# Layer 2 of a four-layer image kernel: the crossing pixel lines copied inside SBUF by ScalarE instead of fetched by transfers

## The chip, the cores and the metric

The kernel runs on one core of a Trainium2 chip. The metric is the device time of one execution in microseconds (us). The kernel before took 3193.68 us, the median of 3 runs (3190.29 to 3196.78). One further execution was profiled; the trace, and every duration read from it, belong to that one.

## The reference

1024 images of 16x16 pixels and 16 channels, float32, pass through four layers, each of the form x = x + layer(groupnorm(x)), with 8 groups of 2 channels:

```python
x = x + _L0_conv_ref(_gn(x), core0, core1, core2)   # a matrix given as a tensor train
x = x + _L1_conv_ref(_gn(x), ...)                   # cellular automaton: Sobel filters, 48->128->16, mask
x = x + _L2_conv_ref(_gn(x), filters, bias)         # 3x3 convolution, 16 -> 16 channels, plus bias
x = x + _L3_conv_ref(_gn(x), ...)                   # cellular automaton again
```

The change is in layer 2 alone: a 3x3 convolution with zero padding at the borders, plus a bias. Each output pixel needs its eight neighbours, so also the pixels one column to the left and right.

## The kernel before

The batch is split into two chunks of 512 images; `X0` and `X1` hold one chunk each in SBUF as [128 partitions, 32 lines, 512 images]. The four layers come one after another, and within a layer chunk 0, then chunk 1. What lies in DRAM between the layers is `xf[layer][chunk]`.

*Layout in layer 2.* A row of an image, 16 columns of 16 channels, is 256 numbers, and a line has only 128 partitions. So the image is cut into a left and a right half (`wh` 0 and 1) of 8 columns: line 16*wh + h holds row h of half wh. Partition 32*m + 2*c + v is column 2*m + v of the half and channel c. All columns of a half are thus on the partition axis, and a 128x128 matrix mixes columns and channels at once.

*The convolution, `layer_conv` (L1138).* For each row h there are two PSUM banks, one a half (6 banks, so three rows can be under way). `inner` (L1160) multiplies lines h-1, h and h+1 of the half by one 128x128 matrix each: three matmuls a half, two at the upper and lower border. In the trace every f32 matmul is two records. The one column that the neighbour half must deliver is not in these lines. `across` (L1169) adds it: a small matmul on a tile `hx`, whose rows 64*wh + 16*y + c hold the other half's border column of row h + y - 1, 48 rows a half. Its output is only the 32 rows of the outermost pair of columns (rows 96 to 127 for the left half, 0 to 31 for the right one). `halo(k)` fills the tile hx for image rows 4k to 4k+3 by DMAs from X to the tile, issued on the sync queue: L1153, and L1156 for the row that the border repeats. There are 48 and 4 of them in the two chunks. Three hx tiles take turns.

*The end of a row, `finish`.* ScalarE (L1191) adds the bias and brings a bank to an SBUF tile r, of which six take turns. GpSimd then issues a DMA (L1192) that adds r onto `xf[2][n]` in DRAM, where x lies already. So the sum x + layer stays in DRAM, and the next user must wait for these transfers.

*What sets the order.* `layer_conv` gives 54 steps: for each pair of rows `first`, `inner`, `first`, `inner`, then `across` for both, then `last` for both. `run` (L1423) goes through them and weaves other work in between: the loads of a list on the sync queue, spread over the first `by` share of the steps, and the steps of a background computation placed by their costs within a span, given as two shares of the layer. On each engine the instructions then run in the order in which they were written. The norms are the background:
- beside the convolution of X0: the 16 loads of X1 (`load_wc`, L766, 512 KB each) and `norm_lines(X1)`: VectorE sums over the lines (L592 and L589), `pmean` on PE (L675), the copy m by ScalarE (L636), 16 subtractions on VectorE (L621), 16 squares by ScalarE (L606) with their sums on VectorE (L592), `pvar` on PE (L679), a reciprocal root (L653, L659 to L663), 16 multiplications (L621);
- beside the convolution of X1: the weights of layer 3 (`put(L3)`), the 16 loads of X0 for layer 3 (`load_cw`, L773) out of what layer 2 has just added up, and `norm_cw(X0)`. That one goes by four quarters of the columns: pmean (L704), m, subtractions, squares and pvar (L708) for each, then one root, then `pr` on PE (L720), which spreads it, and the multiplications by quarter.

The squares' tiles have three buffers, one of which holds the running sum. Layer 3 begins with matmuls on X0 (L1410), whose results ScalarE brings to the tiles hid (L1413), and second matmuls on those (L1263). Layer 1 has the same form; its last operations are L1312 and L1313 on GpSimd and the store L1315 on the sync queue.

Of the kernel before, what the change touches and what calls it, by code (L numbers as in the profile page):

```python
# [12 lines left out]
ALU = mybir.AluOpType  # L13
# [5 lines left out]
B, S, C = 1024, 16, 16  # L19
P = 128  # L20
NB = 512
# [82 lines left out]
def conv_preact_kernel(ctx: ExitStack, tc: tile.TileContext, a: dict, out: bass.AP):  # L104
    nc = tc.nc
    V, A, G, T = nc.vector, nc.scalar, nc.gpsimd, nc.tensor
# [9 lines left out]
    xf = [  # L116
        [dram.tile([8, 4, P, NB], F32, tag=f"xf{l}_{n}", name=f"xf{l}_{n}") for n in range(NCH)]
        for l in range(5)
    ]
# [16 lines left out]
    def work(shape, tag, name, dt=F32):  # L136
        p, sizes = pool["sb"]
        return p.tile(shape, dt, tag=tag, name=name, bufs=sizes[tag])
# [38 lines left out]
    for hf in range(2):  # L177
        rows = slice(64 * hf, 64 * hf + 64)
# [231 lines left out]
    convw = cst("convw", [P, 448])  # L410

    def conv_weights():


        room = work([P, 2, NB], "t4", "convn").rearrange("p a b -> p (a b)")
        fn = room[:, 0:384].rearrange("p (y w o) -> p y w o", y=3, w=8)
        hn = room[:, 384:400]
        fw = convw[:, 0:384].rearrange("p (y w o v) -> p y w o v", y=3, w=4, v=2)
        hw = convw[:, 384:448].rearrange("p (e o v) -> p e o v", e=2, v=2)
        V.memset(room[:, 0:400], 0.0)  # L420
        V.memset(hw, 0.0)
        f = a["L2_conv_filters"]
        with nc.allow_non_contiguous_dma(reason="weights"):
            for w in range(8):
                for kw in range(3):
                    if 0 <= w + kw - 1 < 8:
                        wi = w + kw - 1
                        G.dma_start(
                            fn[32 * (wi // 2) + wi % 2 : 32 * (wi // 2) + 32 : 2, :, w],
                            f[:, kw].rearrange("y i o -> i y o"),  # L430
                        )
            for wh in range(2):
                for y in range(3):
                    r0 = 64 * wh + 16 * y
                    G.dma_start(hn[r0 : r0 + 16], f[y, 2 - 2 * wh])
            for m in range(4):
                for v in range(2):
                    G.dma_start(
                        b2[32 * m + v : 32 * m + 32 : 2], a["L2_conv_bias"].unsqueeze(1)
                    )  # L440

        def spread():
            for y in range(3):
                V.tensor_copy(fw[:, y], fn[:, y].rearrange("p (w v) o -> p w o v", v=2))
            for wh in range(2):
                rows = slice(64 * wh, 64 * wh + 64)
                for e in range(2):
                    V.tensor_copy(hw[rows, e, :, 1 - wh], hn[rows])
                V.memset(hw[64 * wh : 64 * wh + 16, 1], 0.0)

        return spread

# [311 lines left out]
    def load_wc(X, src):  # L764
        return [
            lambda wh=wh, h=h: nc.sync.dma_start(X[:, 16 * wh + h : 16 * wh + h + 2], rows_wc(src, wh, h, 2))  # L766
            for wh in range(2)
            for h in range(0, S, 2)
        ]

    def load_cw(X, src):
        return [
            lambda q=q, w=w: nc.sync.dma_start(  # L773
                X[:, 8 * q + w : 8 * q + w + 2], src[w : w + 2, q].rearrange("w p b -> p w b")
            )
            for q in range(4)
            for w in range(0, 8, 2)
        ]
# [5 lines left out]
    def rows_wc(t, wh, h, n=1):  # L784

        t = t[4 * wh : 4 * wh + 4].rearrange("w q (c h) b -> (w q c) h b", h=S)
        return t[:, h : h + n]
# [182 lines left out]
    def layer_train():  # L970
# [160 lines left out]

    conv = dict(
        fw=convw[:, 0:384].rearrange("p (y m) -> p y m", y=3),
        hw=convw[:, 384:448].rearrange("p (e m) -> p e m", e=2),
    )

    def layer_conv(X, n):

        st = {}

        def start():
            halo(0)

        def halo(k):
            t = st["h", k] = work([P, 4, NB], "hx", "hx")
            for wh in range(2):
                src = X[slice(97, 128, 2) if wh else slice(0, 32, 2), 16 * (1 - wh) : 16 * (1 - wh) + 16]
                for y in range(3):  # L1150
                    r0, h0 = 64 * wh + 16 * y, 4 * k + y - 1
                    lo, hi = max(h0, 0), min(h0 + 4, S)
                    nc.sync.dma_start(t[r0 : r0 + 16, lo - h0 : hi - h0], src[:, lo:hi])  # L1153
                    if lo > h0:

                        nc.sync.dma_start(t[r0 : r0 + 16, 0:1], src[:, 0:1])  # L1156

        def inner(h, y):
            for wh in range(2):
                T.matmul(  # L1160
                    st["po", h][wh], conv["fw"][:, y], X[:, 16 * wh + h + y - 1],
                    start=y == max(0, 1 - h), stop=y == min(2, S - h),
                )

        def across(h):
            rows = 32 if h == S - 1 else 48
            for wh in range(2):
                cols = slice(0, 32) if wh else slice(96, 128)
                T.matmul(  # L1169
                    st["po", h][wh][cols], conv["hw"][64 * wh : 64 * wh + rows, h == 0],  # L1170
                    st["h", h // 4][64 * wh : 64 * wh + rows, h % 4], start=False, stop=False,
                )

        def first(h):
            if h % 2 == 0 and h > 0:
                finish(h - 1)
            if h % 4 == 1 and h + 4 < S:
                halo(h // 4 + 1)
            st["po", h] = [bank([P, NB], "o", "po2") for _ in range(2)]
            inner(h, max(0, 1 - h))  # L1180

        def last(h):
            inner(h, min(2, S - h))
            if h % 2 == 0 or h == S - 1:
                finish(h)

        def finish(h):

            for wh in range(2):
                r = work([P, NB], "r", "conv")  # L1190
                A.activation(r, st["po", h][wh], AF.Identity, bias=b2)  # L1191
                G.dma_start(rows_wc(xf[2][n], wh, h), r.unsqueeze(1), accum_op=ALU.add)  # L1192

        steps = []
        for h in range(0, S, 2):
            for j in (h, h + 1):
                steps.append(lambda j=j: first(j))
                if 0 < j < S - 1:
                    steps.append(lambda j=j: inner(j, 1))
            steps += [  # L1200
                lambda h=h: (across(h), across(h + 1)), lambda h=h: last(h), lambda h=h: last(h + 1)
            ]
        return start, steps
# [219 lines left out]
    def run(layer, us, loads, *spans, by=0.0):  # L1423

        start, main = layer
        start()
        loads, done = list(loads), 0  # L1430
        todo = []
        for bg, lo, hi in spans:
            bg = [b if isinstance(b, tuple) else (1, b) if callable(b) else (b, None) for b in bg]
            idle = sum(b[0] for b in bg if b[1] is None) / (us * (hi - lo))
            less = min(1.0, 0.7 / idle) if idle else 1.0
            weight = sum(b[0] for b in bg if b[1] is not None)
            at = lo
            for cost, step in bg:
                if step is None:
                    at += cost * less / us  # L1440
                else:
                    todo.append((at, step))
                    at += (hi - lo) * (1 - idle * less) * cost / weight
        todo.sort(key=lambda x: x[0])
        for i, step in enumerate(main):
            step()
            part = (i + 1) / len(main)
            while done < len(loads) and done < len(loads) * part / (by or 1e-9):
                loads[done]()
                done += 1  # L1450
            while todo and (todo[0][0] < part or i == len(main) - 1):
                todo.pop(0)[1]()

    def put(L):
        return lambda: nc.sync.dma_start(pack, L["pack"])

    X0, X1 = XN
# [60 lines left out]
    last = alone(N, 3) + rstd(nst, slice(96, 128)) + [3] + scaled(N, [3])  # L1518
    nca_sb = dict(t4=2, s=3, n=2, wq=5, mask=1, f=5, hid=8, u=2, r=4, nx=1)
    nca_ps = dict(h=6, o=2)  # L1520
    conv_sb, conv_ps = dict(gn, s=3, r=6, hx=3), dict(o=6, m=2)
    on_vector[0] = True
    with ExitStack() as es:
        shared[0] = "o"
# [8 lines left out]
    with ExitStack() as es:  # L1533
        shared[0] = "m"
        stage(es, conv_sb, conv_ps)
        run(layer_conv(X0, 0), 108, load_wc(X1, xf[2][1]), (norm_lines(X1), 0.09, 1.1), by=0.12)
        run(
            layer_conv(X1, 1), 108, [put(L3)] + load_cw(X0, xf[3][0]), (norm_cw(X0, True), 0.09, 1.04), by=0.12
        )
    with ExitStack() as es:  # L1540
        shared[0] = "o"
# [41 lines left out]
```

## Time and profile before

| what | value |
|---|---|
| median of 3 runs | 3193.68 us |
| the profiled execution's own time | 3191.8 us |
| its span from first to last instruction | 3190.1 us |
| TensorE clock granted, mean | 0.98 |
| layer 2, first L1160 matmul to the first matmul of layer 3 | 2339.7 to 2591.5 us |
| busy in layer 2: PE, VectorE, ScalarE, GpSimd | 216.8, 158.5, 78.5, 57.1 us |
| L1160: records in layer 2, from start to start | 368, 0.43 us |
| L1169: records, eight in a row | 128, 1.84 us |
| ScalarE: a square of 128x1024 (L606), a result of 128x512 (L1191) | 1.05, 0.69 us |
| VectorE: a subtraction or a sum of 128x1024 in this stage | 1.22 us |
| loads of X1 (L766): first issue | 2349.9 us |
| accumulating transfers of layer 2 (L1192): issue on GpSimd, to landing | 0.95, 6.1 us |

The table's rows are read so. The span is a little less than the execution's own time, and a change inside the span moves both alike. "Busy" is time in which an engine executes an instruction; a PE whose clock is lowered is busy too, only slower. An idle engine costs time only when the work that ends last waits for it. The waits of an engine are named by what ended them: "PE pmean L675 <- DVE s1s L596" is idle time of PE before its matmul into pmean, which ended when VectorE had finished s1s. "SPq" is the sync engine's DMA queue, DVE is VectorE, ACT is ScalarE, POOL is GpSimd, PEld is the loading of weights into TensorE.

### The profile page before, as it was taken

The page shows a single profiled execution, that of the slowest core. Times are in us where ns is not written, and L with a number is a line of the kernel's source. Part 1 is how long each engine was busy: PE and PEld are TensorE (multiplying, and loading weights), DVE is VectorE, ACT ScalarE, POOL GpSimd, SP SyncE. Part 2 cuts the span into 40 slices and gives each one's busy share as a digit, 9 for nine tenths or more (in the row PEclk, how much of TensorE's full clock was granted, in tenths as well). Part 3 has the DMA queues.
Part 4 walks back from the last instruction along what each step waited for, and adds up shares of the span by engine and source line. Part 5 has one row for each costly group of instructions (what it writes and reads, how often), then busy time and mean ns, then how long its engine had stood idle before and what let it go on. Part 6 is the DMA issues. An engine that isn't in the chain of part 4 may idle for free.

```text
span 3190.1 us, 37179 instructions
## 1 busy us (share of the span) xinstructions
PE 3058.5 (96%) x13874; PEld 1260.3 (40%) x13874; DVE 1785.6 (56%) x2378; ACT 1018.3 (32%) x1690; POOL 670.6 (21%) x706
## 2 busy tenths in 40 slices
PE   7899899999999999999999999999979899999996
PEld 5444333444444444444444433333323233333332
DVE  5255345755554555544556678558757647754222
ACT  4331221100001000000111166666624356655553
POOL 1116532200000000000000034435432124432221
PEclk8999999999999999999999999999989999999998
DMA  7535545443333433322222254454476765433445
GB/s 283 201 142 97 121 101 160 133 144 104 104 109 132 146 116 104 104 98 96 90 95 90 76 168 133 129 167 154 139 192 110 185 139 173 136 92 115 128 137 186
DMA packets 243299, 424.77 MB, mean 133 GB/s; under 512 B 37844, under 2 KB 91952, under 8 KB 239408
## 3 DMA queue, kind: packets, MB, share of 16 engines
q1 hardware_dynamic: 217824, 368.63, 35.5%
q0 software_dynamic: 24480, 53.48, 8.3%
q8 instruction: 110, 1.80, 0.2%
q14 instruction: 69, 0.57, 0.1%
q10 hardware_dynamic: 816, 0.30, 0.0%
HBM read 238.78 MB, written 165.60 MB: 127 GB/s over the span
## 4 chain that ended last, share of the span: by engine, by line
issue 46%; PE 31%; POOL 8%; DMA 4%; DVE 2%; SPq 1%; ACT 1%; POOLq 0%; DVEq 0%; ACTq 0%
PE ph L1410 11%; PE po L1078 10%; PE po L1263 4%; POOL res L1313 4%; POOL u L1312 4%; PE po L1160 2%; DMA xn<-xf 1%; PE L_conv_pe L382 1%; SPq L941 1%; DVE xn L621 1%; DMA hx<-xn 1%; PE pw L1001 1%; PE ptout L948 1%; DVE sq L592 1%; POOL L_conv_wy L394 0%
## 5 line engine op out<-in xcount | busy, mean ns | idle before, releaser
L1078 PE MATMUL po<-xn,w 128*128 128x512 f32 x3584 | 1584.3, 598 | 4.6 <-DVE xn L892 4.6
L1078 PEld LDWEIGHTS po<-xn,w 128*128 128x128 f32 x3584 | 669.9, 190 | 852.6 <-issue 833.7
L1413 ACT ACTIVATE hid<-ph,pack 128x512 f32<-128x512 f32 x1024 | 653.9, 686 | 429.2 <-PE ph L1410 308.4
L1114 DVE TENSOR_TENSOR r<-r,po 128x512 f32<-128x512 f32 x576 | 377.8, 683 | 499.0 <-PE po L1078 476.3
L1312 POOL TENSOR_TENSOR u<-u,mask 128x512 f32<-128x512 f32 x128 | 202.5, 1582 | 1858.9 <-DMA nx<-xn 1241.7
L1410 PE MATMUL ph<-xn,wq 32*128 32x512 f32 x3664 | 573.1, 613 | 1.5 <-DMA wq<-L_conv_wy 1.5
L1006 ACT COPY w<-pw 128x512 f32<-128x512 f32 (+1 forms) x320 | 150.6, 558 | 1194.0 <-issue 970.4
L1410 PEld LDWEIGHTS ph<-xn,wq 32*128 32x128 f32 x3664 | 228.6, 184 | 263.3 <-issue 231.4
L1410 PE MATMUL ph<-xn,pack 32*128 32x512 f32 x1288 | 302.2, 631 | 4.5 <-ACT hid L1413 3.2
L1263 PE MATMUL po<-hid,pack 128*32 128x512 f32 x2048 | 283.0, 609 | 1.2 <-DVE u L1275 0.9
L1019 DVE TENSOR_TENSOR w<-w 128x512 f32<-128x512 f32 x320 | 211.2, 684 | 115.2 <-ACT w L1006 114.7
L621 DVE TENSOR_TENSOR xn<-xn,m 128x1024 f32<-128x1024 f32 x160 | 225.9, 1461 | 47.1 <-ACT m L636 47.1
L1313 POOL TENSOR_TENSOR res<-res,u 128x512 f32<-128x512 f32 x128 | 215.2, 1681 | 17.0 <-PE po L1263 2.7
L1275 DVE SCALAR_TENSOR_TENSOR u<-po,pack,xn 128x512 f32<-128x512 f32 x128 | 95.9, 749 | 157.6 <-PE po L1263 150.9
L1160 PE MATMUL po<-xn,convw 128*128 128x512 f32 x368 | 168.5, 609 | 0.0
L1410 PEld LDWEIGHTS ph<-xn,pack 32*128 32x128 f32 x1288 | 114.5, 187 | 100.7 <-issue 61.7
L1114 DVE TENSOR_TENSOR xn<-xn,po 128x512 f32<-128x512 f32 x96 | 64.3, 684 | 125.9 <-PE po L1078 125.8
L592 DVE TENSOR_TENSOR sq<-sq 128x1024 f32<-128x1024 f32 x78 | 110.6, 1418 | 15.2 <-ACT sq L606 12.0
L1263 PEld LDWEIGHTS po<-hid,pack 128*32 128x32 f32 x2048 | 42.9, 108 | 189.7 <-issue 137.4
L394 POOL DMA_DIRECT2D L_conv_wy<-xn x160 | 89.0, 563 | 99.0 <-ACT xn L152 90.7
L1160 PEld LDWEIGHTS po<-xn,convw 128*128 128x128 f32 x368 | 69.3, 193 | 99.3 <-issue 96.7
L592 DVE TENSOR_TENSOR s<-s,xn 128x1024 f32<-128x1024 f32 x60 | 86.4, 1441 | 29.1 <-DMA xn<-xf 27.9
(163 smaller groups left out, 1776.9 us busy)
## 6 DMA issues: line engine op xcount, KB each, us to landing
xf<-r SPq DMA_DIRECT2D x112, 512.0 KB, 3.8
xn<-xf SPq DMA_DIRECT2D x96, 512.0 KB, 5.1
r<-xf SPq DMA_DIRECT2D x80, 512.0 KB, 4.5
wq<-L_conv_wy SPq DMA_DIRECT2D x192, 192.0 KB, 2.8
res<-xf SPq DMA_DIRECT2D x128, 256.0 KB, 3.0
xf<-res SPq DMA_DIRECT2D x96, 256.0 KB, 2.0
res<-xr SPq DMA_DIRECT2D x256, 64.0 KB, 2.8
xf<-conv POOLq DMA_DIRECT2D x64, 256.0 KB, 6.1
```

The source lines that it names most:

```text
L592: return lambda: V.tensor_tensor(st["t"], st["t"], p(), ALU.add)
L621: V.tensor_tensor(part, part, m().unsqueeze(1).broadcast_to([P, 2, NB]), op)
L1006: A.copy(w[:, k0:4, :, 32 * r : 32 * r + 32].rearrange("p k t (v o) -> p v (k t) o", v=2), pw[r],)
L1019: V.tensor_tensor(w[:, k], w[:, x], w[:, y], ALU.add if sign > 0 else ALU.subtract)
L1078: T.matmul(po, st["w", u][:, matrix, t], x, start=t == 0, stop=t == 3)
L1114: V.tensor_tensor(r[at], r[at], po, ALU.add if sign > 0 else ALU.subtract)
L1160: T.matmul(st["po", h][wh], conv["fw"][:, y], X[:, 16 * wh + h + y - 1], start=y == max(0, 1 - h), stop=y == min(2, S - h),)
L1263: T.matmul(po[32 * j : 32 * j + 32], nca["w1"][:, v], hid[j], start=v == 0, stop=v == 1)
L1312: G.tensor_tensor(u, u, st["m"][:, w2], ALU.mult)
L1313: G.tensor_tensor(r, r, u, ALU.add)
L1410: T.matmul(ph, w, x, start=k == 0, stop=k == len(tiles) - 1)
L1413: A.activation(h, ph, AF.Relu, bias=nca["bt"][:, r : r + 1])
```

## The change

- The tile hx holds two image rows for both halves, [96, 2 halves, 2 rows, 512]: rows 32*y to 32*y + 31 are a full pair of columns (both columns, 16 channels) of row h + y - 1. ScalarE fills it with six copies a tile, each 32 partitions by up to 1024 elements, from X's partitions 0 to 31 or 96 to 127. No DMA is left in it. GpSimd clears the row above the upper border in the first tile.
- The weights for it are laid out anew: 96 rows for each half, with zeros for the column of the pair that isn't the neighbour. The matmul of `across` is 96 rows by 32 columns in place of 48 by 32.
- Tiles 0 and 1 are filled at the start of a chunk, tile h/2 + 2 at `first(h)` of each even h, ahead of the `finish` of the row before.
- `finish` puts its accumulating DMAs in a list, from which GpSimd issues them later; twelve r tiles in place of six.
- The loads are spread over the first 0.07 of the steps in place of 0.12, the layer-3 weights come behind the loads of X0, and the norms' spans end at 1.08 and 1.1 in place of 1.1 and 1.04.

```diff
@@ conv_weights
-        hn = room[:, 384:400]
+        hn = room[:, 384:416].rearrange("p (n o) -> p n o", n=2)
...
-                    r0 = 64 * wh + 16 * y
-                    G.dma_start(hn[r0 : r0 + 16], f[y, 2 - 2 * wh])
+                    G.dma_start(hn[32 * y + wh : 32 * y + 32 : 2, wh], f[y, 2 - 2 * wh])
...
-                rows = slice(64 * wh, 64 * wh + 64)
-                for e in range(2):
-                    V.tensor_copy(hw[rows, e, :, 1 - wh], hn[rows])
-                V.memset(hw[64 * wh : 64 * wh + 16, 1], 0.0)
+                V.tensor_copy(hw[:, wh, :, 1 - wh], hn[:, wh])
@@ layer_conv
         def start():
             halo(0)
+            halo(1)
 
         def halo(k):
-            t = st["h", k] = work([P, 4, NB], "hx", "hx")
-            for wh in range(2):
-                src = X[slice(97, 128, 2) if wh else slice(0, 32, 2), 16 * (1 - wh) : 16 * (1 - wh) + 16]
-                for y in range(3):
-                    r0, h0 = 64 * wh + 16 * y, 4 * k + y - 1
-                    lo, hi = max(h0, 0), min(h0 + 4, S)
-                    nc.sync.dma_start(t[r0 : r0 + 16, lo - h0 : hi - h0], src[:, lo:hi])
-                    if lo > h0:
-
-                        nc.sync.dma_start(t[r0 : r0 + 16, 0:1], src[:, 0:1])
+            if k >= S // 2:
+                return
+            t = st["h", k] = work([96, 2, 2, NB], "hx", "hx")
+            if k == 0:
+                G.memset(t[0:32, :, 0], 0.0)
+            for y in range(3):
+                lo, hi = max(2 * k + y - 1, 0), min(2 * k + y + 1, S)
+                at = lo - (2 * k + y - 1)
+                for wh in range(2):
+                    A.copy(
+                        t[32 * y : 32 * y + 32, wh, at : at + hi - lo],
+                        X[96 * wh : 96 * wh + 32, 16 * (1 - wh) + lo : 16 * (1 - wh) + hi],
+                    )
@@
         def across(h):
-            rows = 32 if h == S - 1 else 48
+            rows = slice(0, 64 if h == S - 1 else 96)
             for wh in range(2):
                 cols = slice(0, 32) if wh else slice(96, 128)
                 T.matmul(
-                    st["po", h][wh][cols], conv["hw"][64 * wh : 64 * wh + rows, h == 0],
-                    st["h", h // 4][64 * wh : 64 * wh + rows, h % 4], start=False, stop=False,
+                    st["po", h][wh][cols], conv["hw"][rows, wh], st["h", h // 2][rows, wh, h % 2],
+                    start=False, stop=False,
                 )
 
         def first(h):
-            if h % 2 == 0 and h > 0:
-                finish(h - 1)
-            if h % 4 == 1 and h + 4 < S:
-                halo(h // 4 + 1)
+            if h % 2 == 0:
+                halo(h // 2 + 2)
+                if h > 0:
+                    finish(h - 1)
@@
+        waiting = []
+
         def finish(h):
 
             for wh in range(2):
                 r = work([P, NB], "r", "conv")
                 A.activation(r, st["po", h][wh], AF.Identity, bias=b2)
-                G.dma_start(rows_wc(xf[2][n], wh, h), r.unsqueeze(1), accum_op=ALU.add)
+                waiting.append((rows_wc(xf[2][n], wh, h), r.unsqueeze(1)))
+            while waiting and 2 * h + 2 - len(waiting) < 4 * (h - 4):
+                G.dma_start(*waiting.pop(0), accum_op=ALU.add)
@@ the stages
-    conv_sb, conv_ps = dict(gn, s=3, r=6, hx=3), dict(o=6, m=2)
+    conv_sb, conv_ps = dict(gn, s=3, r=12, hx=3), dict(o=6, m=2)
...
-        run(layer_conv(X0, 0), 108, load_wc(X1, xf[2][1]), (norm_lines(X1), 0.09, 1.1), by=0.12)
+        run(layer_conv(X0, 0), 108, load_wc(X1, xf[2][1]), (norm_lines(X1), 0.09, 1.08), by=0.07)
         run(
-            layer_conv(X1, 1), 108, [put(L3)] + load_cw(X0, xf[3][0]), (norm_cw(X0, True), 0.09, 1.04), by=0.12
+            layer_conv(X1, 1), 108, load_cw(X0, xf[3][0]) + [put(L3)], (norm_cw(X0, True), 0.09, 1.1), by=0.07
         )
```

More of the change, by code (lines that the diff above doesn't have):

```diff
@@ L416, in conv_weights @@
         fn = room[:, 0:384].rearrange("p (y w o) -> p y w o", y=3, w=8)
-        hn = room[:, 384:400]
+        hn = room[:, 384:416].rearrange("p (n o) -> p n o", n=2)
         fw = convw[:, 0:384].rearrange("p (y w o v) -> p y w o v", y=3, w=4, v=2)
-        hw = convw[:, 384:448].rearrange("p (e o v) -> p e o v", e=2, v=2)
-        V.memset(room[:, 0:400], 0.0)
+        hw = convw[:, 384:448].rearrange("p (n o v) -> p n o v", n=2, v=2)
+        V.memset(room[:, 0:416], 0.0)
         V.memset(hw, 0.0)
@@ L1133, in conv_preact_kernel @@
         fw=convw[:, 0:384].rearrange("p (y m) -> p y m", y=3),
-        hw=convw[:, 384:448].rearrange("p (e m) -> p e m", e=2),
+        hw=convw[:, 384:448].rearrange("p (n m) -> p n m", n=2),
     )
```

## The prediction, made before the changed kernel ran

> **What bounds the kernel now.** I read the page's head and slices first, then the stage's own windows, its waits on PE, and last the chain of waits within it. The slices say that TensorE is the bound nearly everywhere, with a dip in slices 30 to 32, where the clock granted falls too:
>
> ```profile
> span 3190.1 us, 37179 instructions
> ...
> PE 3058.5 (96%) x13874; PEld 1260.3 (40%) x13874; DVE 1785.6 (56%) x2378; ACT 1018.3 (32%) x1690; POOL 670.6 (21%) x706
> ...
> PE   7899899999999999999999999999979899999996
> ...
> PEclk8999999999999999999999999999989999999998
> ```
>
> The dip is the layer-2 stage, 2339.7 to 2591.5 us. The windows show where in it PE stands (columns: window, length, busy time of each engine with its instructions, clock, DMA share, GB/s):
>
> ```profile
> 2339.70:2357.00 17.30, 11.10 (x22) 3.21 (x22) 3.60 (x4) 0.00 (x0) 3.33 (x2) 0.80 0.68 182
> 2357.00:2381.00 24.00, 24.00 (x56) 9.75 (x55) 10.81 (x9) 5.50 (x8) 6.98 (x8) 0.93 1.04 275
> 2381.00:2399.00 18.00, 5.59 (x13) 1.32 (x12) 7.02 (x7) 0.00 (x0) 0.00 (x0) 0.62 1.07 236
> 2399.00:2464.00 65.00, 64.43 (x166) 25.03 (x166) 57.48 (x51) 31.90 (x41) 18.65 (x22) 1.00 0.63 97
> 2464.00:2480.00 16.00, 15.97 (x41) 6.18 (x39) 5.77 (x6) 3.55 (x6) 5.67 (x7) 1.00 1.00 207
> 2480.00:2493.00 13.00, 2.06 (x3) 1.03 (x4) 4.38 (x5) 0.00 (x0) 0.00 (x0) 0.63 1.07 330
> 2493.00:2591.50 98.50, 93.61 (x233) 33.30 (x232) 69.43 (x64) 37.50 (x51) 22.47 (x26) 0.98 0.63 122
> ```
>
> Three holes: about 6 us at the start, 12.4 of the third row, 11 of the sixth. The waits on PE name them:
>
> ```profile
> PE pmean L675 <- DVE s1s L596: 12.4, 1, 12.4
> PE pmean L704 <- DVE s1s L596: 11.0, 1, 11.0
> PE po L1169 <- DMA hx<-xn: 6.2, 2, 5.4
> PE pvar L708 <- DVE s2s L596: 4.9, 2, 2.6
> ```
>
> Both pmean holes are a channel sum that waits for the loads of the other chunk, at a DMA share of 1.0. The chain of waits shows the crossing lines' own transfers between those loads, 12.56 and 6.25 us long:
>
> ```profile
> 2364.36 18.16 DMA xn<-xf
> 2382.53 12.56 DMA hx<-xn
> 2395.11 6.25 DMA hx<-xn
> 2402.03 18.25 DVE xn L621 x16
> ```
>
> So the stage is 251.8 us, of which PE needs some 202 (368 records of L1160 at 0.43 from start to start, 128 of L1169 at 0.23, 28 of the norms), and about 50 us is waiting or slow clock.
>
> **What the Trainium skill says.** "ScalarE: Activation LUTs", section "What ACT_TABLE_LOAD costs": an ACTIVATE with immediate operands takes 186 ns + 0.833 ns an element, and neighbours overlap by some 93 ns; for 1024 elements that is an estimate of 0.95 us each in a row. The trace agrees: squares of 128x1024 follow each other by 0.94 (three in 2.94 us with a full tail). "TensorE: Matmul & The Clock Gate", Part 1: after an idle window of about 3.4 us the array runs at half rate, and needs as long of work to recover. The trace agrees: clock 0.62 in the rows with 11 and 12 us gaps, 1.00 and 0.98 in those whose gaps are at most 2.6. "TensorEngine Tiling (Array Packing)", section "Key Properties": different tiles can load and multiply in parallel. The trace has it for four tiles of 128 rows by 32 columns: L1263 gives 8 records in 1.07 us.
>
> **The change, part by part.** All against the profiled execution (3191.8 us, span 3190.1), which lies 1.9 below the median 3193.68.
>
> *Removed:* 52 transfers into hx, each 0.51 to 0.58 us of the sync queue, and their share of the DMA engines. The first loads of X1 go out behind the L1315 store at 2344.9 instead of 2349.9, and all 16 together. By the 390 GB/s that loads reach alone (387 to 395 in the slices at 2481 to 2494) one costs 1.34 us, so 10 are in by about 2361, when the first result's accumulate (1.73 us of all engines each: 41.7% of 265 us over 64) starts to share. The other six end between 2372 and 2376; before, 2391.7. PE reaches pmean at about 2376 and no longer waits there: 15 to 17 us gained at that point.
>
> *Added on ScalarE:* 6 copies a block, 32x1024, at 0.94 to 0.95 (taken from the square row; not below 0.85, the bare 0.833 an element, not above 1.22, what VectorE takes for L621 of the same 1024 columns). A block is 5.7 us, the first and last of a chunk 4.8, a chunk 45 us. ScalarE's 78 us in the stage become about 168 of 250: on average it has room. But its instructions run in program order, and the order puts blocks 0, 1 and 2 (18 copies) ahead of the first finish(0), and blocks 3 to 7 between the later finishes, mean copies (L636) and squares (L606).
> - Start of chunk 0: block 0 can't begin before the last L1312/L1313 pair has freed the room that hx takes, 2343.1. It ends 2348.0, 1 at 2353.7, 2 at 2359.5, finish(0) 2360.8. PE has 6 banks, three rows; the crossing matmuls wait until 2348 (before 2350.5), and first(3) waits from 2356.8 to 2360.2 for finish(0), 3.4 us. Those two cancel, and pmean is then due anyway when the loads are.
> - m after pmean: behind a finish pair and block 4, so 2382 (before 2402). Subtractions, 16 in 18.25: until 2400.4. Squares after: their adds take 16 x 1.3 = 20.8 us on VectorE, and the row of ScalarE, in which finish(8), block 7 and finish(9) stand between the squares, starves them by 5.6. s2s at about 2429, before 2441.7. PE stands before pvar from 2418.6 to 2429, 10.4 us that are new, and comes out cold (+2.7, as before after the 11 us gap: pmean 2.08 in place of 1.04, four matmuls 3.4 in place of 1.9). Chunk 0 ends at about 2455.4; before 2464: **gain 8.6**.
> - Chunk 1: the loads of X0 still wait for the landing of the last accumulate, so they go with the chunk's end. Blocks 0 to 2 run 2455.4 to 2472.9, first(3) waits 3.5. pmean of the first quarter is at 2475.5 to 2476.4 (before 2493.0): ahead by **16**. From here ScalarE's row takes it back. m waits behind block 3 and finish(1): 2481.8, ahead by only 11.8. pvar of quarter 0 stalls 8.0 us (squares behind block 4 and finish(3)), quarter 1 7.9 (behind block 5), quarter 2 3.5, quarter 3 none; the two long ones each leave PE cold, +2.7. That is 24.8, where before the pvar stalls were 4.9. So 16 - (24.8 - 4.9) = -3.9, of which some 5 comes back, because the rows near the end, which stood behind VectorE's m and pr copies, now wait less. The last matmul of the stage ends at about 2589.2 (before 2590.5), and the first quarter that layer 3 needs is multiplied by 2590.6: **-1.5**.
> - Layer 3's start: the second hid activation waits for the landing of the last accumulate, where before it needed row 13's or 14's: +1 at worst, 0 at best.
>
> *Added on GpSimd:* a memset (about 0.5 us, as its other 16x512 memset) ahead of nothing that waits at that time; 0. The results held in `waiting`: in the program's order GpSimd still issues the same accumulates one after another, each waiting for its activation; nothing else is in its queue for them to be held behind. Cost and gain 0. Twelve r buffers in place of six: an activation could wait for an accumulate six behind; L1191 shows only PE waits (123.2 of 123.4 us idle), so 0.
>
> *Crossing matmuls:* 96 rows in a 128x32 tile in place of 48 in a 64x32 one. The pair of halves differ in columns, and if they overlap as L1263's do they still cost 0.23 us a record; if not, 0.43, +25 us for 128 records. I take 0: L1263's rows are the same tile shape at one quarter of the time.
>
> *Windows and load order* (1.1 to 1.08, 1.04 to 1.1, by 0.12 to 0.07, put(L3) behind the loads): the loads were due early already, and the weights of layer 3 aren't needed before 2591; the later end of the norm of X0 is in the row above. The conversion of the weights is outside the stage, 6 transfers as before: 0.
>
> Sum: 0 for the start, -8.6 for chunk 0, of which chunk 1 gives back 7.1: **-1.5 us**, bounds by the copies' price below. From the median: 3192.0.
>
> **Rivals.**
> (a) *The gain stays (faster).* If chunk 1 runs at the pace of PE from the first pmean on, as 2493 to 2591 did before (98.5 us with 4.9 of stalls), the 16 us gained at pmean remain, less the 3.5 that first(3) waits: about -13, 3180.5. For: ScalarE has 80 us to spare on average, and the stalls I count depend on an order in which a block could well pass in PE's shadow. Against: m and the squares stand behind blocks of 5.7 us while two square buffers hold VectorE for only 2.6.
> (b) *ScalarE's row becomes the bound (slower).* Some nine blocks lie on the path: four in chunk 0 and five in chunk 1. Each tenth of a us on a copy adds 6 x 9 x 0.1 = 5.4 us. At 1.05 a copy (the mean of one square, with no overlap) the sum is +4.4; it turns slower by more than 0.2% from 1.09 on; at 1.15 it is +9.9, 3203.6. For: copies that change partitions are in no row of the trace. Against: squares and L1191 overlap in a row.
> (c) *Crossing tiles don't overlap:* +25, 3217. Against: L1263. Chance small.
> (d) *Nothing moves:* the results held are a no-op; but the halo isn't, since the DMA row vanishes.
>
> **How the numbers follow.** The ledger's case 0.42, its own range 3187 to 3198 (copies 0.90 to 1.03); (a) 0.34; (b) 0.21; (c) 0.03. I can tell no less than 0.2% (6.4 us) from no change. Faster: (a) and a little of the ledger's low end, 0.37. Slower: (b), (c), 0.23. Same: 0.40. The range goes from (a)'s 3180.5 less 2.5, 3178, to (b)'s 3204; outside it are (c) and the tails, under 0.2.
>
> **What would show it.** Right: no DMA into hx, loads of X1 from 2345; PE reaches pmean L675 without a wait, and the one-time 11 us wait of L704 is gone; new waits of PE on s2s (L679 about 10, L708 two of about 8), on finish(0) 3.4 twice, clock down in those; ScalarE busy 168 us. Wrong: waits of L708 below 3 us (then (a)), copies above 1.09 (then (b)), L1169 records at 0.43 apart (then (c)), GpSimd's accumulates in a different order.

## The result, and the profile after

The changed kernel took 3214.6 us (median of 4 runs, 3209.6 to 3218.3), the kernel before on the same chip 3195.2 (3190.3 to 3201.0). The ratio is 1.0059, with a 95% interval from 1.0036 to 1.0082: 19 us slower, 12 to 26. The prediction had 3192.0, and a range that ended at 3204. The profiled execution took 3212.4 us, its span is 3210.7.

The lines of PE and its clock on the page after show the dip where it was, a slice or two later and as deep:

```profile
span 3210.7 us, 37203 instructions
...
PE 3072.1 (96%) x13874; PEld 1264.6 (39%) x13874; DVE 1785.7 (56%) x2374; ACT 1114.0 (35%) x1786; POOL 672.6 (21%) x708
...
PE   7899899999999999999999999999998799999996
...
PEclk8899999999999999999999999999999899999998
```

The windows of the stage after, cut at places that answer to those of before (2463.6 is the end of chunk 0, 2602.3 the first matmul of layer 3); the first, and the one from 2383 to 2401.6, in which PE is busy throughout, are left out:

```profile
2359.60:2383.00 23.40, 18.96 (x42) 7.42 (x41) 12.21 (x11) 21.69 (x25) 5.67 (x7) 0.85 0.88 242
...
2401.60:2463.60 62.00, 51.19 (x128) 19.77 (x127) 48.03 (x43) 38.39 (x46) 14.26 (x17) 0.92 0.49 68
2463.60:2480.00 16.40, 15.14 (x37) 5.44 (x35) 5.77 (x6) 16.07 (x17) 2.95 (x4) 1.00 0.99 259
2480.00:2493.00 13.00, 9.80 (x19) 3.59 (x20) 5.84 (x7) 11.55 (x14) 3.47 (x4) 0.74 1.06 351
2493.00:2602.30 109.30, 90.55 (x214) 32.90 (x212) 60.86 (x56) 60.45 (x73) 22.27 (x26) 0.92 0.47 77
```

The two large holes at the sums are gone: PE is busy all the time from 2383 to 2401.6, in the row left out, where it was idle for 12 us before, and 9.8 of 13 us from 2480 on, where it was 2.1. In their place PE stands for 11 us in the rest of chunk 0 (2401.6 to 2463.6), and the last row has grown from 98.5 to 109.3 us. ScalarE, the fourth of the busy times, is at work for nearly all of the rows from 2359.6, 2463.6 and 2480. The waits of PE after (from 2339 to 2620 us) say for whom:

```profile
PE pvar L704 <- DVE s2s L592: 18.8, 3, 8.0
PE pvar L675 <- DVE s2s L592: 10.8, 1, 10.8
PE po L1160 <- ACT conv L1193: 8.9, 2, 4.4
PE po L1169 <- ACT hx L1153: 2.6, 1, 2.6
```

The lines of the program have other numbers after: L1193 is the result (L1191 before), L671 and L675 are pmean and pvar of X1 (L675 and L679), L700 and L704 those of the quarters (L704 and L708), L588 and L592 the sums, L602 the squares, L617 the subtractions.

No wait for s1s or for a transfer into hx is left. But 41 us of waits for squares, for the results of the first row and for copies have come, against 35 us before. One quarter of chunk 1 shows what lies behind a wait for s2s. These are lines of the timeline after (start, length, engine, what, and in brackets the idle time before it and what ended that):

```profile
2495.16 2.94 ACT L602 ACTIVATE sq<-xn 128x1024 f32<-128x1024 f32 x3
...
2498.00 6.30 ACT L1153 COPY hx<-xn 32x1024 f32<-32x1024 f32 x6
2504.32 1.27 ACT L1193 ACTIVATE conv<-po,b 128x512 f32<-128x512 f32 x2
...
2505.47 1.05 ACT L602 ACTIVATE sq<-xn 128x1024 f32<-128x1024 f32 x1
2506.56 1.23 DVE L588 TENSOR_TENSOR sq<-sq 128x1024 f32<-128x1024 f32 x1 [6.82 <-ACT sq L602]
...
2508.64 1.91 PE L704 MATMUL pvar<-s2s,gv_cw 128*32 128x512 f32 x2 [7.24 <-DVE s2s L592]
```

Three of the quarter's four squares are done at 2498.1; the fourth stands behind a block of copies and two results, so VectorE waits 6.8 us for it and PE 7.2, and the pvar that follows takes 1.91 us in place of 1.04, because the clock has fallen: from 2508 to 2512 the granted share is 0.50.

Where the time went, by the start of the same work in both profiles. The stage begins 2.6 us later after, for reasons that lie before it (from run to run that place moved by -2.4 to +4.3 us); the last column takes that off.

| work | before | after | difference within the stage |
|---|---|---|---|
| first matmul of L1160 | 2339.7 | 2342.3 | 0 |
| s1s of X1 is ready | 2393.8 | 2374.0 | -22.4 |
| pmean of X1 on PE | 2393.9 | 2383.1 | -13.4 |
| pvar of X1 on PE | 2441.7 | 2437.4 | -6.9 |
| pmean of quarter 0 on PE | 2490.9 | 2486.8 | -6.7 |
| first matmul of layer 3 | 2591.5 | 2602.3 | +8.2 |
| its first second matmul (L1263, L1267) | 2598.0 | 2613.6 | +13.0 |

The loads' part of the change came: s1s is 22 us earlier. Each later line gives a piece of it back.

### The profile page after: what moved, and what is told of

It reads as the page before. It is cut to its first block, busy times and chain, and to the rows that moved or that the text cites. A ratio compares the mean times of both kernels' runs of the same rounds, so it can differ in the third digit from the quotient of the medians.

```text
span 3210.7 us, 37203 instructions
## 1 busy us (share of the span) xinstructions
PE 3072.1 (96%) x13874; PEld 1264.6 (39%) x13874; DVE 1785.7 (56%) x2374; ACT 1114.0 (35%) x1786; POOL 672.6 (21%) x708
## 4 chain that ended last, share of the span: by engine, by line
issue 50%; PE 27%; POOL 10%; ACT 2%; DVE 1%; DMA 1%; SPq 1%; POOLq 0%; DVEq 0%; ACTq 0%
PE po L1074 10%; PE ph L1414 7%; POOL u L1316 5%; POOL res L1317 5%; PE po L1160 3%; PE po L1267 3%; PE L_conv_pe L382 1%; ACT hx L1153 1%; DVE sq L588 1%; PE po L1169 1%; PE ptout L944 1%; PE pw L997 1%; SPq L937 1%; POOL L_conv_wy L394 0%; DMA xn<-xf 0%
## 5 line engine op out<-in xcount | busy, mean ns | idle before, releaser
L1267 PE MATMUL po<-hid,pack 128*32 128x512 f32 x2048 | 285.2, 614 | 0.7 <-DVE u L1279 0.4
L617 DVE TENSOR_TENSOR xn<-xn,m 128x1024 f32<-128x1024 f32 x160 | 225.5, 1458 | 60.4 <-ACT m L632 60.3
L1160 PE MATMUL po<-xn,convw 128*128 128x512 f32 x368 | 173.2, 624 | 8.9 <-ACT conv L1193 8.9
L588 DVE TENSOR_TENSOR sq<-sq 128x1024 f32<-128x1024 f32 x78 | 110.7, 1419 | 40.4 <-ACT sq L602 37.1
L1267 PEld LDWEIGHTS po<-hid,pack 128*32 128x32 f32 x2048 | 43.1, 109 | 190.2 <-issue 139.3
L1160 PEld LDWEIGHTS po<-xn,convw 128*128 128x128 f32 x368 | 71.8, 200 | 112.6 <-issue 98.9
L1153 ACT COPY hx<-xn 32x1024 f32<-32x1024 f32 (+1 forms) x96 | 96.5, 1005 | 5.6 <-POOL u L1316 4.5
```

What stands on the lines that cost most here:

```text
L588: return lambda: V.tensor_tensor(st["t"], st["t"], p(), ALU.add)
L617: V.tensor_tensor(part, part, m().unsqueeze(1).broadcast_to([P, 2, NB]), op)
L1160: T.matmul(st["po", h][wh], conv["fw"][:, y], X[:, 16 * wh + h + y - 1], start=y == max(0, 1 - h), stop=y == min(2, S - h),)
L1267: T.matmul(po[32 * j : 32 * j + 32], nca["w1"][:, v], hid[j], start=v == 0, stop=v == 1)
```

## The experiments

The theory after the result, A: ScalarE works in the order of the program, and the copies keep it from the results, the means and the squares that PE and VectorE wait for. Rivals: B, the held results and the twelve r tiles delay the accumulates and layer 3's start; C, the spans that end later; D, PE's own work with 96 rows; E, that transfers and loads share the DMA engines, whatever the queue. All times are medians, and ratios are to the kernel before on the same chip.

### The copies alone (e2_halo_alone)

```diff
-    conv_sb, conv_ps = dict(gn, s=3, r=12, hx=3), ...
+    conv_sb, conv_ps = dict(gn, s=3, r=6, hx=3), ...
-                waiting.append(...)   # and the loop that issues from the list
+                G.dma_start(rows_wc(xf[2][n], wh, h), r.unsqueeze(1), accum_op=ALU.add)
-        run(layer_conv(X0, 0), 108, ..., (norm_lines(X1), 0.09, 1.08), by=0.07)   # and X1: 1.1, put(L3) last
+        run(layer_conv(X0, 0), 108, ..., (norm_lines(X1), 0.09, 1.1), by=0.12)    # and X1: 1.04, put(L3) first
```

> The ScalarE halo with its 96-row weights alone; the results go out as before (six r tiles, no list), spans and loads as before. Theory A (ScalarE's order: the copies stand ahead of the results, means and squares that PE and VectorE wait for): the halo carries all of the loss, so 3210 to 3219 us, within 5 of the changed kernel. Rival B (the held results and twelve r tiles delay the accumulates and the next layer's start): this one is faster than the changed kernel by 4 us or more, 3200 to 3210. Rival C (the spans that end later cost it): also faster than the changed kernel, and pmean of the quarters comes earlier after its sums.

Measured: 3212.7, ratio 1.0050 (1.0038 to 1.0062), 16 us slower than before. The halo carries the loss; the rest of the change is worth at most a few us either way. In the profile the quarter's means do come earlier with these spans, as C says (within the stage, pmean of quarter 1 is 9.5 us ahead of before, where the changed kernel is level), and the stage's last pr is 4 us earlier than in the changed kernel; but layer 3's start gives that back: its second hid waits 4.7 us for the landing of an accumulate.

### The copies later (e3_late), and with the old spans (e12_late_spans)

```diff
         def first(h):
             if h % 2 == 0:
-                halo(h // 2 + 2)
                 if h > 0:
                     finish(h - 1)
+                    halo(h // 2 + 1)
```

> Only where the copies stand is changed: 12 in place of 18 ahead of a chunk's first result, and each later block behind the two results of the row before, one pair of rows later. Theory A: the two waits of PE for the first result (4.4 us each, with 2.8 and 1.9 us of slow clock behind them) go away, and some of the waits for s2s get shorter; 14 us less than the changed kernel at most, 3198 to 3207. If the length of ScalarE's work mattered and not its place, nothing would change: 3214.

> e3_late (all copies by ScalarE, one pair later, behind the results) with the spans and the order of loads of the kernel before. The spans apart from the split: 3200 to 3203 if they are worth 4 us where ScalarE is full, 3204 to 3207 if they are worth nothing. Not below the kernel before in any case, if ScalarE's 100 us of copies are what costs.

Measured: 3205.7, ratio 1.0037 (1.0023 to 1.0051); with the old spans 3202.4, ratio 1.0022 (1.0014 to 1.0031). The waits of e3_late:

```profile
PE pvar L704 <- DVE s2s L592: 24.9, 3, 12.3
PE pvar L675 <- DVE s2s L592: 11.8, 1, 11.8
PE pmean L671 <- DVE s1s L592: 6.2, 1, 6.2
...
PE po L1160 <- ACT conv L1193: 0.2, 1, 0.2
```

The wait for the first result went from 8.9 to 0.2 us as meant. But it was not won: PE now comes to s1s 6.2 us early, and the waits for s2s grew by 7. At layer 3's start this kernel is no earlier in its stage than the changed one: its first matmul comes 11.8 us later than before (8.2 in the changed kernel), its first L1267 14.0 (13.0), and 80 us into layer 3 both are 14.0 us late. So where the 9 us of the medians were gained isn't shown by the two profiles; it isn't in the stage. Theory A is too narrow: to move a block moves the wait. The old spans help here by some 5 us more (the two intervals overlap). In the profiles the first L1267 comes 6 us earlier with them, of which 2.7 us are left 80 us into layer 3.

### Fewer copies (e5_one_tile, e14_one_tile_chunk1) and shorter ones (e13_half_copies)

```diff
+            if k > 0:                     # e14: if k > 0 and n == 1
+                st["h", k] = st["h", 0]
+                return
```

> Only tile 0 of each chunk is filled, and all rows multiply by it: 7 of 8 blocks of copies are left out, so the crossing pixels of rows 2 to 15 are not the reference's; the matmuls stay. It prices the copies. Theory A: the waits for the first result and for s2s go, the gain of the earlier loads stays: 3180 to 3190 us, less than the kernel before. Rival D (the 96-row matmuls): stays above 3205. Rival B (held results, r tiles): stays by about 4 us above what A says, with layer 3's start still waiting for the last accumulate; a bit of B is in A's upper end.

> The changed kernel; tile 0 alone is filled in chunk 1, all tiles in chunk 0. The crossing pixels of rows 2 to 15 of chunk 1 are not the reference's. Without the copies of both chunks (e5_one_tile) it was 41 us less than the changed kernel. By the chain of that comparison chunk 0 carries about 9 of it and chunk 1 the rest: 3180 to 3188. If chunk 0's lateness were made up in chunk 1 it would be 3173, and if chunk 0 carried half, 3194.

```diff
-                        t[32 * y : 32 * y + 32, wh, at : at + hi - lo],
-                        X[96 * wh : 96 * wh + 32, 16 * (1 - wh) + lo : 16 * (1 - wh) + hi],
+                        t[32 * y : 32 * y + 32, wh, 0:1],
+                        X[96 * wh : 96 * wh + 32, 16 * (1 - wh) + lo : 16 * (1 - wh) + lo + 1],
...   # and in across: st["h", h // 2][rows, wh, 0] in place of [rows, wh, h % 2]
```

> The changed kernel with each copy cut to one image row of the two, 32x512 in place of 32x1024; both rows of a pair multiply by it, so the crossing pixels of the odd rows are not the reference's. Number, places and waits of the copies stay. A copy follows the next by 0.63 in place of 1.055. The prediction's rule (5.4 us for each 0.1 us on a copy) says 23 us less, 3191. If the waits end before that, because a block of 3.8 us already fits beside PE's work, it is 3180 to 3186. If the number of instructions or their waits were the cost, it would stay above 3205.

Measured: without the copies of tiles 1 to 7, 3173.8, ratio 0.9934 (0.9921 to 0.9947); without those of chunk 1 alone, 3188.0, ratio 0.9975 (0.9967 to 0.9984); with all copies at half length, 3189.0, ratio 0.9975 (0.9968 to 0.9982). The waits of e5_one_tile:

```profile
PE pvar L704 <- DVE s2s L592: 8.8, 2, 6.6
PE pmean L671 <- DVE s1s L592: 6.3, 1, 6.3
...
PE pvar L675 <- DVE s2s L592: 2.2, 1, 2.2
```

So the copies cost (1.0059 - 0.9934) x 3195 = 40 us, some 27 of it in chunk 1 and 13 in chunk 0, and what is left of the change without them is 21 us faster than the kernel before. Not every wait for s2s comes from the copies: 11 us of them stay in e5 (5.5 before). D is out: these kernels have the 96-row matmuls. It is the time of the copies and not their number or waits: 96 copies at 0.62 us cost 13 us over e5, the same 96 at 1.04 cost 40. The second half of each copy is worth 27 us, 6.3 for each 0.1 us; the first half far less. So blocks of 3.8 us still cost 13 us, and blocks of 6.3 us three times that.

### Other engines and queues (e4_gpsimd, e8_halo_act_queue)

```diff
-                    A.copy(
+                    G.tensor_copy(
                         t[32 * y : 32 * y + 32, wh, at : at + hi - lo],
```

> The same 96 copies by GpSimd in place of ScalarE, at the same places in the program. No row shows a copy of 32x1024 by GpSimd; its multiplication of 128x512 takes 1.58 us (L1316), its memset of 32x1024 1.14. Theory A: ScalarE's waits vanish. If a copy takes up to 1.9 us, a block of six fits into a pair of rows (12.3 us of PE) and the time is 3185 to 3196; from 2 us on the blocks, with the accumulates queued behind them, are the bound and it is 3215 or more. Rival D (96 rows or the tile of two rows cost PE itself): stays at 3214 whatever the copy takes.

The other one starts from the kernel before:

```diff
-                    nc.sync.dma_start(t[r0 : r0 + 16, lo - h0 : hi - h0], src[:, lo:hi])
+                    nc.scalar.dma_start(t[r0 : r0 + 16, lo - h0 : hi - h0], src[:, lo:hi])   # and L1156
```

> The kernel before, with the transfers into hx issued on ScalarE's DMA queue in place of the sync queue, so that the loads of X1 go out at about 2345 and neither stands behind the other. No copies, 48 rows. Theory A (what holds the changed kernel back is ScalarE's time, and the gain sought is the loads' earlier start): the 52 issues cost ScalarE about 0.5 us each, 26 us where the copies cost 100; 3180 to 3192, faster than before. Rival E (the transfers share the DMA engines with the loads, and that, not the queue's order, delays pmean): within 4 us of before, 3192 to 3200.

Measured: copies by GpSimd 3205.0, ratio 1.0023 (1.0015 to 1.0031), between the two cases: a copy takes 1.92 us at the median, but from 0.6 (half of the length) to 7.4. ScalarE has no copy here, and still 21.9 us of waits for s2s are left (9.6 and 12.3, in the changed kernel 10.8 and 18.8). The sums of the squares and of the loads on VectorE show why, first in this kernel and then in e5_one_tile:

```profile
L588 DVE TENSOR_TENSOR sq<-sq 128x1024 f32<-128x1024 f32 x27 | 45.2, 1676 | 2.8 <-ACT sq L602 0.6
L588 DVE TENSOR_TENSOR s<-s,xn 128x1024 f32<-128x1024 f32 x22 | 40.8, 1854 | 1.3 <-DMA xn<-xf 0.5
...
L588 DVE TENSOR_TENSOR sq<-sq 128x1024 f32<-128x1024 f32 x27 | 33.1, 1225 | 8.4 <-ACT sq L602 6.4
L588 DVE TENSOR_TENSOR s<-s,xn 128x1024 f32<-128x1024 f32 x22 | 27.0, 1225 | 13.2 <-DMA xn<-xf 12.6
```

VectorE's operations of 128x1024 take 1.94 us at the median while GpSimd copies throughout, and 1.22 while it doesn't. GpSimd's copies take 1.92 at the median while VectorE is at work throughout, and 1.03 while it is idle. So the two slow each other, and the copies, taken off ScalarE, delay the same sums by way of VectorE.

Transfers on ScalarE's queue: 3214.2, ratio 1.0059 (1.0045 to 1.0072), 19 us slower, which neither theory had. The lines of hx in this kernel: who waited for its transfers, and what the issues themselves waited for:

```profile
  DMA hx<-xn: 89.4, 10
...
  ACT conv L1191: 46.1, 2
  PE po L1169: 41.8, 4
```

The issues on ScalarE stood still for 89 us, each until an earlier transfer had landed. The view puts these waits down to transfers into hx. But the program counts the transfers of the sync queue and of ScalarE's queue together, on eight semaphores in turn, and in chunk 0 five of the issues start 0.02 to 0.03 us after the landing of a load of X1 whose semaphore they take. The loads of X1 did go out at 2345, but the transfers into hx, taken off the sync queue, wait for those loads all the same, and ScalarE's results stand behind them. E is neither shown nor refuted by it. The queue alone was never what tied the two together.

### The form of the copy (e7_activation)

```diff
-                    A.copy(
+                    A.activation(
...
+                        AF.Copy,
```

> The changed kernel with the 96 copies written as an activation (Copy) in place of the copy instruction; places and sizes stay. The copies of 32x1024 follow each other by 1.055 us, where squares of 128x1024 follow by 0.945. If the form of the instruction sets that, the copies follow by 0.95, and by the prediction's rule (5.4 us for each 0.1 on a copy) the time falls by 5 to 6 us, 3207 to 3210. If it is the 32 partitions or the operands, nothing changes: 3212 to 3217, and the 0.94 of the prediction was never to be had.

Measured: 3214.4, ratio 1.0055 (1.0042 to 1.0068), as the changed kernel. The line of these copies among those of hx:

```profile
L1153 ACT ACTIVATE hx<-xn x96: 614/1055/1062, 2346.1 to 2572.3; 32x1024 f32<-32x1024 f32 x88, 32x512 f32<-32x512 f32 x8
```

From start to start they take 1.07 us. The form of the instruction isn't what keeps these copies from overlapping as squares do. Whether the 32 partitions do, or something else in the operands, stays open.

### The r tiles (e9_r8)

```diff
-    conv_sb, conv_ps = dict(gn, s=3, r=12, hx=3), ...     # and the list of held results
+    conv_sb, conv_ps = dict(gn, s=3, r=8, hx=3), ...
```

> The changed kernel with eight r tiles in place of twelve and no list of held results. In its program the second hid of layer 3 waits for the landing of row 14's transfer, not of the last one. Theory A with the landing as a small part: 1 to 4 us less than the changed kernel, 3210 to 3214, PE's wait for hid at layer 3's start gone. Rival B (the held results cost more than that): 3206 or less. If twelve tiles and the list helped: over 3217.

Measured: 3207.6, ratio 1.0037 (1.0025 to 1.0048), some 6 us less than e7_activation on the same chip, though the two intervals overlap a little. In the stage the two profiles agree within 0.5 us up to the last pr, so holding the results neither helped nor harmed there. The difference begins at layer 3's second hid, which in e7_activation has this line in the timeline:

```profile
2610.70 4.23 ACT L1418 ACTIVATE hid<-ph,pack 128x512 f32<-128x512 f32 x7 [5.13 <-DMA xf<-conv]
```

It waits for the last result's accumulate to land, since its tile takes the room of that result's r tile. With eight tiles, another one lies there. From the last pr to 80 us into layer 3, e7 loses 5.6 us and e9 1.5. The changed kernel loses only 2.2 there, though its second hid waits as well:

```profile
2610.04 4.16 ACT L1417 ACTIVATE hid<-ph,pack 128x512 f32<-128x512 f32 x7 [4.91 <-PE ph L1414]
```

The view names PE, but the last accumulate lands 0.1 us before this start, as it does in e7. Within its stage the hid comes 1.0 us later than in e9. What e7 has beyond that is a slow clock right behind the wait, which lasts twice as long (6.8 us, against 3.4 before it in the other two). The executions profiled of e7 and e9 are 0.9 us apart in all, so the 6 us of the medians are measured, but their place is not shown.

### Half of the copies by GpSimd (e10_split_late, e11_split_late_spans)

```diff
                 if h > 0:
                     finish(h - 1)
+                    halo(h // 2 + 1)     # in place of halo(h // 2 + 2) ahead of finish
...
-                    A.copy(
+                    (G.tensor_copy if wh else A.copy)(
```

> As e3_late (copies one pair of rows later, behind the results), and half of the copies, those for the right half, by GpSimd. A block of ScalarE is then 3.15 us in place of 6.3[...]. GpSimd's three copies of 1.9 us take 5.8 of the 12.3 us of a pair. Theory A: the waits for s2s fall to 3 us or less each, and the time is 3185 to 3195, at or below the kernel before. If copying on both at once slows each other or VectorE, or GpSimd's accumulates come late, 3200 and more.

> e10_split_late (copies one pair later, behind the results, half of them by GpSimd) with the spans and the order of loads of the kernel before. In e2_halo_alone, which has those spans, the pmean of quarter 1 came 13 us earlier than in the changed kernel and the stage ended some 4 us earlier. If the later spans (1.1 for the norm of X0) cost that much: 4 us less than e10, 3183 to 3188, the fastest complete kernel. If the spans only matter where ScalarE is full: 3188 to 3193 as e10.

Measured: 3190.2, ratio 0.9985 (0.9977 to 0.9993), and with the old spans 3188.9, ratio 0.9977 (0.9970 to 0.9984): 5 and 7 us faster than the kernel before. This pair tells the spans' worth where ScalarE has room: about 2 us, or nothing, since the intervals overlap. The copies and the waits for s2s in e11:

```profile
L1153 ACT COPY hx<-xn x48: 600/1042/1046, 2345.2 to 2562.3; 32x1024 f32<-32x1024 f32 x44, 32x512 f32<-32x512 f32 x4
L1153 POOL COPY hx<-xn x48: 604/1037/2060, 2347.4 to 2563.7; 32x1024 f32<-32x1024 f32 x44, 32x512 f32<-32x512 f32 x4
```

```profile
PE pvar L704 <- DVE s2s L592: 13.6, 3, 6.2
PE pvar L675 <- DVE s2s L592: 6.6, 1, 6.6
```

The waits for s2s are 20.2 us, where e12, alike but for the split, has 34.1. I had expected 3 us or less for each, and they are up to 6.6. GpSimd's copies slow VectorE here too: its 22 sums of the loads take 34.8 us, in the changed kernel 27.0. The gap to e5's 3174 says that copies shared in this way aren't free; how much of it is ScalarE's half and how much GpSimd's isn't shown.

## Why the prediction was wrong, step by step

*What bounded the kernel, and the loads.* Right. With the transfers into hx gone, the loads go out behind L1315 and s1s is ready 22 us earlier; the forecast had 15 to 17 at pmean. e5 shows the worth of that with hardly any copies: 21 us, where rival (a) had 13.

*ScalarE's order.* Right in its mechanism, and the waits for s2s nearly to the tenth: forecast 10.4, 8.0, 7.9, 3.5; measured 10.8, 7.2, 8.0, 3.5. The blocks of copies were longer than forecast, 6.3 us for 5.7, so that the numbers agree this well is in part luck.

*"Those two cancel, and pmean is then due anyway when the loads are."* This step failed, and it is the largest part: it set the wait for the first result at 3.4 us with no slow clock behind it. At the start of chunk 0 the copies, the first result and PE's next rows stand so in the timeline after:

```profile
2345.72 18.18 ACT L1153 COPY hx<-xn 32x512 f32<-32x512 f32 x18 [4.45 <-POOL u L1316]
...
2363.92 1.27 ACT L1193 ACTIVATE conv<-po,b 128x512 f32<-128x512 f32 x2
...
2364.66 6.26 PE L1160 MATMUL po<-xn,convw 128*128 128x512 f32 x8 [4.44 <-ACT conv L1193]
...
2373.29 0.69 DVE L592 TENSOR_TENSOR s1s<-s 128x512 f32<-128x512 f32 x1
...
2383.10 1.02 PE L671 MATMUL pmean<-s1s,gm_wc 128*128 128x512 f32 x2
```

s1s was there at 2374; PE wasn't, until 2383. It had waited 4.4 us for the first result and not 3.4, and then ran slowly: 8 matmuls in 6.26 us, 3.44 when warm. I had put a slow clock behind the long waits alone, and none behind this one. The Trainium skill ("TensorE: Matmul & The Clock Gate", Part 1) has an idle window of about 3.4 us as the limit, and my 3.4 sat on it; the measured 4.4 lies above, and the trace has the slow clock behind it, in both chunks: 0.51 granted from 2364.7 to 2370 us, 0.50 from 2483.2 to 2489. The wait of 3.5 us for s2s of quarter 2, forecast as 3.5 without a slow clock, had one behind it too (pvar 1.86 us in place of 1.04). So pmean of X1 gained 13 us where PE could have had 22, and in chunk 1 pmean of quarter 0 came 6.7 us ahead of before, not 16. Of these 9 us, about 2 are the two longer waits and about 4.6 the slow clock behind them (2.8 in chunk 0, and 1.8 in chunk 1 up to this matmul); the other 2.5 or so fit to longer copies.

*The price of a copy.* Mis-sized: 0.94 forecast, 1.055 from start to start. The Trainium skill ("ScalarE: Activation LUTs", "What ACT_TABLE_LOAD costs") has neighbours overlap by 93 ns. Squares of 128 partitions do; these copies of 32 don't, nor do the activations in their place in e7_activation, and for them the measurement decides. The rule in rival (b), 5.4 us for each 0.1, held: 6.3 between half and full length. But it puts only some 6 of the 20 us that were missed on the price. It also makes rival (b) half right: the mechanism was that one, and the loss came below the 1.09 from which it was to decide, because the sum that it started from was too low. The price's part overlaps with that of the waits above, which are made of copies.

*From there to layer 3.* Nearly right as a sum: from pmean of quarter 0 to the first matmul of layer 3 the stage loses 14.9 us, forecast 14.5. By the starts of the same matmuls of L1160 it is at most 10.9 us late and at its end 8.2, so some 2.7 came back, forecast 5.

*Layer 3's start, "+1 at worst".* Too small as a whole: from its first matmul to 80 us later another 5.7 us are lost. The wait for the last accumulate's landing, which this step was about, is 1.0 of them by the start of the second hid in the changed kernel and in e9_r8, as forecast; against e7_activation's profile it is 4. e9 loses 5.0 there without that wait. In the kernels with the later spans the last pr stands beside layer 3's first matmuls, and from those to the first L1267 it takes 8.6 us and more, where before, e11 and e12, with the old spans, have 6.4. At 80 us the old spans are 2.7 (e12 against e3) and 3.6 us ahead (e11 against e10) in the profiles. So the later end of the norm of X0, to which the prediction gave no price here, is likely a good part of it; that isn't shown for the changed kernel itself.

*The rest.* 96 rows in a 128x32 tile cost nothing: eight records still take 1.91 us. The held results are a no-op within the stage, as forecast (e9). The spans, which I put at nothing apart from the row of chunk 1, cost some 5 us where ScalarE is full (e3 against e12, with overlapping intervals) and 2 or nothing where it isn't (e10 against e11).

In the profiled pair the miss is 22 us: 9 up to pmean of quarter 0, under 1 from there to layer 3, 5 to 6 at its start, 2.6 before the stage and 4 behind it. The last two weren't followed up; the place of the stage moves by as much between profiles of other kernels.

## What to carry to other kernels

When work is moved to an engine with time to spare, its mean load says little: write down its program order, and find which of the other engines' waits end behind the moved block. To put the block elsewhere in that order moved the wait here; to make it shorter (e13), or share it with a second engine (e11 against e12), cut the waits for s2s to some 20 us, from 30 and 34. The second engine can have a price of its own: GpSimd's copies slowed VectorE. And price a wait of PE that may be followed by a slow clock together with the slow work behind it: of what was missed at the first results, the slow work was the larger part, 4.6 us against 2.

## What was not expected of the hardware

- Copies of 32 partitions by 1024 on ScalarE follow each other by 1.055 us, squares of 128 by 1024 by 0.945.
- The same copy on GpSimd takes 1.03 us while VectorE is idle and 1.92 at the median while VectorE is at work throughout (e4; 1.03 and 1.92 in e11 too). VectorE's operations of 128x1024 take 1.94 us while GpSimd copies, and 1.22 otherwise.
- Transfers issued on the sync queue and on ScalarE's still wait for each other, through the eight semaphores on which this program counts both (89 us of standing issues in e8). GpSimd's accumulates are counted on others.
